# A four-layer graph network on one core: attention of twelve node tiles from a slot array, one one-hot of four on ScalarE, weights' sums by fours of node tiles

## The chip, the cores and the metric

One core of a Trainium2 chip runs the whole program as one launch. The metric is the device time of one execution in microseconds. Five engines work side by side: PE (matmuls; its weight loads are listed as PEld), DVE (VectorE), ACT (ScalarE), POOL (GpSimd) and SP (SyncE, which here only issues DMAs). Indirect gathers and stores (one row per partition, the row numbers taken from a column in SBUF) are issued from POOL, plain DMAs from SP and some from ACT.

## The reference

12,500 nodes with 96 features, 200,000 edges sorted by destination, 96 edge attributes. Four layers, each with a residual and a layer norm. Layers 0, 1 (two steps inside) and 3 sum rows of the source nodes over the edges of each destination; layer 2 is attention over edges with 8 heads of 12:

```python
x = _layernorm(x + _L0_gnn_ref(x, src, dst, ...))        # x@W_self + mean of x[src] @ W_neigh
x = _layernorm(x + _L1_gnn_ref(x, ..., src, dst))        # twice: sums of (x@W0)[src], then x / std
# _L2_gnn_ref:
Q_h, K_h, V_h = ((x @ Wq + bq), (x @ Wk + bk), (x @ Wv + bv))   # as (N, 8, 12)
E = (edge_attr @ We + be).reshape(-1, H, D)
score = K_h[src] * Q_h[dst] / sqrt(D) * E
score = exp(clip(score.sum(-1, keepdims=True), -5.0, 5.0))
wV = segment_sum(V_h[src] * score, dst);  Z = segment_sum(score, dst)
h_out = wV / (Z + 1e-06)
x = _layernorm(x + h_out)
x = _layernorm(x + _L3_gnn_ref(x, src, dst, ...))        # softmax-weighted sums of relu(x[src])
```

## The kernel before

**Tiles.** There are 98 node tiles of 128 nodes (`NB`) and 1563 edge tiles of 128 edges in the order of their destinations (`NT`). The edges of node tile d lie in the edge tiles `reach(d)`, 16d-6 to 16d+21.

**Two ways to sum over edges.** *By slots*: for the first 76 node tiles (`NS`) the first stage sorts each node tile's edges into 25 slot tiles of 128 places (`SQ`, 3200 places, `SD`), so that a group of 32 places holds edges whose sources all lie in one node tile. Source rows then come from a table in SBUF by matmuls with a one-hot `ohT` (four matmuls of 32 columns per slot tile, called granules), and a second one-hot `ohd` sums them into the node tile. 64 edges per node tile that do not fit are gathered as spare rows. Both one-hots are stored in DRAM (`ohT_d`, `ohd_d`) and loaded again by later passes. *By edges*: for the other node tiles POOL gathers source rows with an indirect DMA for each edge tile (`by_edges`, L1389), and one-hots made on DVE sum them.

**Stages.** (1) `passes`, first part: `edge_block` and `edge_steps` order the edges in 20 steps of 64 edge tiles, mostly on DVE; `first_sums` follows them, one node tile a turn (it makes and stores the one-hots, L1206 to L1225, gathers that tile's spare row on POOL, L1245, runs the granules on PE, L1302, and the sums, L1316); `by_edges` is advanced beside it. The framework's scheduler orders the instructions of this stage on each engine. (2), (3) Two `whole_pass` runs for the two steps of layer 1; the second also stores keys and values as f32 rows (`kv_d`) and queries as two f16 halves (`q_d`). (4) `attention`, wholly by edges. (5) `whole_pass` for layer 3, by slots for 68 node tiles, with its table of four f16 parts held in SBUF, where attention's `stage` writes it.

**Attention.** 391 units of four edge tiles. The order of work on PE, DVE, ACT and POOL is written out by hand (`manual_schedule`): round u asks for the key and value rows of unit u+8 (`ask`, L1631: four indirect gathers on POOL into one of 12 buffers `kv`), fetches the edge attributes and query rows of unit u+4 (SP), and does `score(u)`, `weigh(u-1)`, `terms(u-2)` with `one_hots_of(u-2)`, `queries(u+3)`, one step of the node stage, and `scatter(u-3)`. `score` has eight matmuls for the edge terms (f32, two passes, `ep`, L1669), eight for the queries (`qp`, L1673), two multiplications on DVE (`s`, L1677 and L1678) and the sum over each head (`sc`, L1680). `weigh` takes the exponential on ACT (L1689) and multiplies the values on DVE (`m`, L1692); with that a `kv` buffer comes free. `terms` splits the result into two f16 halves (`mh`, L1701, L1702); `one_hots_of` makes four one-hots of 256 columns on DVE (`ohe`, L1709); `scatter` sums into the node tiles (`acc`, L1725, seven matmuls a unit). `done` closes each node tile on DVE: the two halves' sum, the weights' sum, its reciprocal, a product (L1738 to L1743).

Of the kernel before, what the change touches and what calls it, by code (L numbers as in the profile page):

```python
# [11 lines left out]
F32 = mybir.dt.float32  # L12
# [11 lines left out]
P = 128  # L24
# [506 lines left out]
NS3 = 68  # L531
TS = 16 * NS + 8
# [10 lines left out]
def gnn_fast(  # L543
# [67 lines left out]
    kv_d = dram.tile([NB * P, 2 * D], F32, name="kv_d")  # L611
    q_d = dram.tile([(NB + 1) * P, 2 * D], F16, name="q_d")
# [192 lines left out]
    def l0_nodes(work, psum, pieces):  # L805
# [3 lines left out]
        for g, n in node_batches():  # L809
            xg = work.tile([P, GB, D], F32, name="x0", bufs=2)  # L810
# [11 lines left out]
            own = work.tile([P, GB, D], F32, name="own0", bufs=2)  # L822
# [32 lines left out]
    def edge_constants(big):  # L855
# [7 lines left out]
        c.first = big.tile([P, NT], BF16, name="first")  # L863
        c.cont = big.tile([P, NT], BF16, name="cont")
        c.same = big.tile([P, NT], BF16, name="same")
# [16 lines left out]
        with tc.tile_pool(name="s_ord", bufs=1) as ordp, tc.tile_pool(name="s_ordp", bufs=2, space=PSUM) as psum:  # L882
# [24 lines left out]
            last = ordp.tile([P, NT], F32, name="last")  # L907
            for j0 in range(0, NT, 512):
                n = min(512, NT - j0)
                for k, to in enumerate((c.first, last)):  # L910
                    p = psum.tile([P, 512], F32, name="p")
                    nc.tensor.matmul(p[:, :n], ones_f[0:1, :], ends[:, k, j0 : j0 + n], start=True, stop=True)
                    nc.vector.tensor_copy(to[:, j0 : j0 + n], p[:, :n])
            nc.vector.memset(c.cont[:, 0:1], 0.0)
            nc.vector.tensor_tensor(c.cont[:, 1:], c.first[:, 1:], last[:, : NT - 1], op=ALU.is_equal)
# [30 lines left out]
    def edge_block(c, blk, psum, b0):  # L946
# [27 lines left out]
        if slots:  # L974
# [4 lines left out]
            t.rearrange("t (f i) -> t f i", i=4), rowf[:, 1].rearrange("t i f -> t f i"),  # L979
# [65 lines left out]
        b.j = blk.tile([P, BL], F32, name="j")  # L1045
# [7 lines left out]
    def edge_steps(c, work, psum, t0):  # L1053
# [80 lines left out]
        pg_all = pb.rearrange("p k (g i) -> p k g i", i=UE)  # L1134

# [41 lines left out]

    def expand(work, psum, placed, d):
# [3 lines left out]
        p = psum.tile([SQ, P], F32, name="tp")  # L1182
        nc.tensor.transpose(p, lo[:, :SQ], ident)
        r = work.tile([SQ, P], BF16, name="lorow", bufs=2)
        nc.scalar.copy(r, p)
        nc.scalar.dma_start(rowd[d], r)
# [363 lines left out]
    def l1_stage(i):  # L1550
        def stage(work, psum, g, n, sums):
# [32 lines left out]
            nc.sync.dma_start(rows(kv_d, g, n), kv[:, :n, :])  # L1584
            nc.sync.dma_start(
# [6 lines left out]
    def attention():  # L1592
# [4 lines left out]
        CQ = 16  # L1597
        with ExitStack() as c2:
            cols, within = by_columns(c2.enter_context(tc.tile_pool(name="e_cols", bufs=1)), 0, NT, F32)
# [4 lines left out]
            accp = c2.enter_context(tc.tile_pool(name="e_acc", bufs=3, space=PSUM))  # L1604
            five = one.tile([P, per, HEADS], F32, name="five")
            nc.vector.memset(five, 5.0)
            wide = one.tile([P, 2 * P], BF16, name="wide")
            nc.gpsimd.iota(wide, pattern=[[1, 2 * P]], base=1, channel_multiplier=0, allow_small_or_imprecise_dtypes=True)
            attr = []
            for i in range(6):  # L1610
                t = one.tile([D + 1, per * P], F32, name=f"attr{i}")
                nc.vector.memset(t[D : D + 1], 1.0)
                attr.append(t)
            units = [(t0, min(per, NT - t0)) for t0 in range(0, NT, per)]
            blocks, got, asked, early, acc, held = {}, {}, {}, {}, {}, {}

            def ask_block(b):
                if b * CQ < NT:
                    n = min(CQ, NT - b * CQ)
                    qb = work.tile([P, CQ * P], BF16, name="qb")  # L1620
# [3 lines left out]
            def ask(u):  # L1624

                if u >= len(units):
                    return
                t0, n = units[u]
                kv = uw.tile([P, per, 2 * D], F32, name="kv", bufs=EARLY + 4)
                for i in range(n):  # L1630
                    nc.gpsimd.indirect_dma_start(  # L1631
                        out=kv[:, i, :], out_offset=None, in_=kv_d,
                        in_offset=bass.IndirectOffsetOnAxis(ap=cols[:, t0 + i : t0 + i + 1], axis=0),
# [3 lines left out]
            def fetch(u):  # L1637
# [4 lines left out]
                if t0 % CQ == 0:  # L1642
# [7 lines left out]
            def queries(u):  # L1650
# [4 lines left out]
                b = blocks[t0 // CQ][:, t0 % CQ * P : (t0 % CQ + n) * P]  # L1655
# [5 lines left out]

            def score(u):
                t0, n = units[u]
                a, qs = got.pop(u)
                ohq = asked.pop(u)
                kv = early.pop(u)
                ep = psum.tile([P, per, D], F32, name="ep")
                for i in range(n):
                    nc.tensor.matmul(ep[:, i, :], a[:, i * P : (i + 1) * P], w_e, start=True, stop=True)  # L1669
                qp = psum.tile([P, per, D], F32, name="qp")  # L1670
                for i in range(n):
# [4 lines left out]
                s = uw.tile([P, per, D], F32, name="s")  # L1676
                nc.vector.tensor_mul(s[:, :n, :], ep[:, :n, :], kv[:, :n, :D])  # L1677
                nc.vector.tensor_mul(s[:, :n, :], s[:, :n, :], qp[:, :n, :])  # L1678
                sc = uw.tile([P, per, HEADS], F32, name="sc", bufs=3)
                nc.vector.tensor_reduce(sc[:, :n, :], s[:, :n, :].rearrange("p e (h d) -> p e h d", d=HD), AX.X, ALU.add)  # L1680
                nc.vector.scalar_tensor_tensor(  # L1681
                    sc[:, :n, :], sc[:, :n, :], -5.0, five[:, :n, :], op0=ALU.max, op1=ALU.min
                )
                return n, kv, sc

            def weigh(n, kv, sc):
# [3 lines left out]
                m = uw.tile([P, per, HEADS, H1], F32, name="m")  # L1690
                nc.scalar.mul(m[:, :n, :, HD], ex[:, :n, :], 2.0**8)
                nc.vector.tensor_mul(  # L1692
                    m[:, :n, :, :HD], kv[:, :n, D:].rearrange("p e (h d) -> p e h d", d=HD),
                    ex[:, :n, :, None].to_broadcast([P, n, HEADS, HD]),
                )
                return n, m.rearrange("p e h d -> p e (h d)")

            def terms(n, m):
# [4 lines left out]
                return mh  # L1703

            def one_hots_of(u):
                t0, n = units[u]
                o = uw.tile([P, per, 2 * P], BF16, name="ohe")
# [284 lines left out]
```

## Time and profile before

| | us |
|---|---|
| median of 3 runs | 7493.61 (7463.65 to 7509.52) |
| profiled execution | 7481.49, its span 7479.0 |
| stage 1, with its start | 0 to 1541 |
| pass one, pass two | 1541 to 2550, 2550 to 3512 |
| attention | 3512 to 6098 |
| last pass | 6098 to 7479 |

The stage bounds are where the first and last instructions of each stage's lines start in the trace. Busy time of an engine counts when an instruction of it runs; matmuls overlap and their ends are modelled, so PE's busy time is not a measure of how full it is. A line of waits says which instruction waited, whose end released it, and then the total, the number and the longest of these waits. "issue" means that the profile shows nothing that was waited for, "remote" that the release can't be put down to an instruction.

### The profile page before, as it was taken

The numbers are of one execution on the slowest core, as the hardware profiler recorded it, in microseconds if no ns is written. First come the engines' busy times: TensorE is split into PE (matmuls) and PEld (weight loads), VectorE is DVE, ScalarE is ACT, GpSimd is POOL, SyncE is SP. The second block draws the span as 40 slices with busy tenths as digits, with TensorE's granted clock in tenths as the row PEclk, the third lists the DMA queues.
The fourth block names the chain that finished last, engine by engine and source line by source line (L and its number), as shares of the span: only waits on it lengthen the run. The fifth ranks groups of instructions, "written<-read, shape, count | busy, mean of one in ns | idle before, by whom it ended". The sixth has DMA issues, their size and how long they took to land.

```text
span 7479.0 us, 155826 instructions
## 1 busy us (share of the span) xinstructions
PE 4678.3 (63%) x63527; PEld 3383.4 (45%) x63527; DVE 4144.3 (55%) x9827; ACT 2805.1 (38%) x5549; POOL 3381.0 (45%) x3338
## 2 busy tenths in 40 slices
PE   5666666746667566676445555555555547777777
PEld 3455545534445444445344444444444434444344
DVE  7577777723334344445466666666666654454445
ACT  2455455522323223334234443334433433333334
POOL 0443454334343344332666656666665643334331
PEclk8677778767777777777565656655656558787788
DMA  4545455543333333344344444444444432233222
GB/s 106 155 162 167 147 173 166 169 107 101 105 101 110 102 109 113 108 119 140 111 124 131 126 125 130 127 127 128 127 129 126 127 91 87 88 91 87 87 88 66
DMA packets 656950, 894.03 MB, mean 120 GB/s; under 512 B 394162, under 2 KB 458885, under 8 KB 651357
## 3 DMA queue, kind: packets, MB, share of 16 engines
q1 hardware_dynamic: 498742, 615.02, 26.4%
q0 software_dynamic: 138784, 262.63, 13.2%
q8 instruction: 500, 8.19, 0.4%
q10 hardware_dynamic: 18695, 6.32, 0.4%
q14 instruction: 229, 1.88, 0.1%
HBM read 747.72 MB, written 135.87 MB: 118 GB/s over the span
## 4 chain that ended last, share of the span: by engine, by line
PE 31%; DVE 22%; another core or an unknown queue 17%; issue 16%; POOL 5%; ACT 4%; DMA 2%; DVEq 0%; ACTq 0%; SPq 0%; POOLq 0%
PE rows L1444 9%; PE acc L1455 8%; POOL kv L1631 5%; PE acc L1373 3%; DVE ohe L1709 3%; DVE msg L1447 2%; PE acc L1316 2%; DVE s L1678 2%; PE rows L1302 2%; DVE sc L1680 2%; DVE mh L1702 2%; DVE s L1677 2%; ACT msg L1306 1%; PE place L1166 1%
## 5 line engine op out<-in xcount | busy, mean ns | idle before, releaser
L1631 POOL DMA_INDIRECT kv<-kv_d,cols x1563 | 1543.3, 987 | 987.8 <-DVE m L1692 521.9
L1447 ACT CAST msg<-rows 128x384 f16<-128x384 f32 (+1 forms) x1440 | 876.7, 641 | 1810.6 <-remote 1110.7
L1444 PE MATMUL rows<-tab,ohT 128*32 128x192 f16 (+1 forms) x21560 | 1122.9, 294 | 677.6 <-issue 588.4
L1447 DVE CAST msg<-rows 128x768 f16<-128x768 f32 x720 | 687.3, 955 | 1486.7 <-remote 1027.4
L1389 POOL DMA_INDIRECT rows_e<-tab_d,cols x1065 | 1128.3, 1059 | 628.3 <-PE acc L1373 323.1
L1444 PEld LDWEIGHTS <-ohT 128*32 128x32 fp8e4 x21560 | 598.1, 101 | 1106.8 <-issue 1027.9
L1455 PE MATMUL acc<-msg,ohd 128*32 128x384 f16 (+1 forms) x10600 | 928.2, 323 | 260.1 <-issue 254.9
L1725 PE MATMUL acc<-mh,ohe 128*128 128x208 f16 x2727 | 516.1, 352 | 845.6 <-DVE ohe L1709 592.2
L1455 PEld LDWEIGHTS <-ohd 128*32 128x32 fp8e4 (+1 forms) x10600 | 558.8, 103 | 534.7 <-issue 441.3
L1725 PEld LDWEIGHTS <-ohe 128*128 128x128 bf16 x2727 | 294.3, 125 | 1008.3 <-DVE ohe L1709 648.0
L1669 PE MATMUL ep<-w_e,attr 97*128 97x96 f32 x3126 | 653.3, 378 | 22.9 <-issue 17.6
L1689 ACT ACTIVATE ex<-sc 128x32 f32<-128x32 f32 x391 | 89.6, 229 | 1477.9 <-DVE sc L1681 1255.6
L1389 POOL DMA_INDIRECT rows_e<-ex_d,cols x483 | 465.1, 963 | 384.8 <-PE acc L1373 246.2
L1669 PEld LDWEIGHTS ep<-w_e,attr 97*128 97x128 f32 x3126 | 621.6, 293 | 26.2 <-issue 13.3
L1673 PE MATMUL qp<-qs,ohq 128*128 128x96 f16 x3126 | 357.5, 258 | 345.1 <-issue 325.5
L1677 DVE TENSOR_TENSOR s<-ep,kv 128x384 f32<-128x384 f32 x391 | 216.1, 553 | 638.7 <-remote 446.6
L1306 ACT CAST msg<-rows 128x768 f16<-128x768 f32 x633 | 386.0, 644 | 428.8 <-PE rows L1302 186.3
L1316 PE MATMUL acc<-msg,ohd 128*32 128x194 f16 x7600 | 381.6, 291 | 242.3 <-ACT msg L1306 156.4
L1673 PEld LDWEIGHTS <-ohq 128*128 128x128 fp8e4 x3126 | 293.7, 134 | 396.6 <-issue 393.2
L1302 PE MATMUL rows<-tab,ohT 128*32 128x192 f16 x7448 | 395.2, 287 | 76.7 <-issue 74.9
L1245 POOL DMA_INDIRECT spare<-tab_d,spare_i x76 | 130.8, 1721 | 653.5 <-PE rows L1302 365.1
L1254 POOL DMA_INDIRECT spare<-tab_d,spare x76 | 72.4, 953 | 731.1 <-PE rows L1444 613.2
(695 smaller groups left out, 7566.9 us busy)
## 6 DMA issues: line engine op xcount, KB each, us to landing
ohT<-ohT_d SPq DMA_DIRECT2D x220, 400.0 KB
ohd<-ohd_d SPq DMA_DIRECT2D x220, 400.0 KB
attr<-cols_edge_attr_dram SPq DMA_DIRECT2D x390, 192.0 KB
bc<-rowd SPq DMA_DIRECT2D x76, 800.0 KB
qb<-qrow SPq DMA_DIRECT2D x97, 512.0 KB
sb<-srow SPq DMA_DIRECT2D x38, 1024.0 KB
ohd_d<-ohd SPq DMA_DIRECT2D x76, 400.0 KB
ohT_d<-ohT SPq DMA_DIRECT2D x76, 400.0 KB
```

Source lines behind the costliest of these rows:

```text
L1302: nc.tensor.matmul(ps[j * GR : (j + 1) * GR, i // R, i % R * W : (i % R + 1) * W], a, b, start=True, stop=True)
L1306: nc.scalar.copy(m[:, : n * R].rearrange("p (b r) t w -> p b (r t) w", r=R)[:, :, :, :D], ps[:, :n, : R * W].rearrange("p b (t w) -> p b t ...
L1316: nc.tensor.matmul(acc[d][j : j + GR, : W + 2], got[d][1][:, q, j : j + GR], m, start=(q == 0), stop=(q == SQ - 1))
L1389: nc.gpsimd.indirect_dma_start(out=m[:, i, :W], out_offset=None, in_=table, in_offset=bass.IndirectOffsetOnAxis(ap=rest_src[:, t : t + 1], ...
L1444: nc.tensor.matmul(ps[j * GR : (j + 1) * GR, i // R, i % R * W : (i % R + 1) * W], a, b, start=True, stop=True)
L1447: (nc.scalar.copy if engine else nc.vector.tensor_copy)(m, ps[:, :, : R * W])
L1455: nc.tensor.matmul(acc[d][j : j + wide, :W], got[d][1][:, q, j : j + wide], m, start=(q == 0), stop=(q == SQ - 1))
L1631: nc.gpsimd.indirect_dma_start(out=kv[:, i, :], out_offset=None, in_=kv_d, in_offset=bass.IndirectOffsetOnAxis(ap=cols[:, t0 + i : t0 + i ...
L1669: nc.tensor.matmul(ep[:, i, :], a[:, i * P : (i + 1) * P], w_e, start=True, stop=True)
L1673: nc.tensor.matmul(qp[:, i, :], ohq[:, i * P : (i + 1) * P], qs[:, t * D : (t + 1) * D], start=(t == 0), stop=(t == 1))
L1677: nc.vector.tensor_mul(s[:, :n, :], ep[:, :n, :], kv[:, :n, :D])
L1725: nc.tensor.matmul(acc[d].rearrange("p t w -> p (t w)"), ohe[:, i, k * P : (k + 1) * P], m[:, i].rearrange("p t w -> p (t w)"), start=(t = ...
```

## The change

- **Twelve node tiles by slots (`MS = 12`).** Attention's unit list becomes 345 edge units from edge tile 184 on, and 75 slot units of four slot tiles, spread evenly over them from the 16th edge unit to 24 before the end. A slot unit takes key and value rows (f16 halves) by granules from a table in SBUF, query rows by a one-hot made from a row of places' destinations, and edge terms from a slot array `es_d`.
- **The slot array.** The first stage fills `es_d` with zeros (three DMAs), works out each edge's place (`slot_i`), and after step 3 puts in, turn by turn, the edge terms of four of the first 198 edge tiles (`edge_terms`), with one indirect store per edge tile from POOL.
- **The table.** Pass two also stores keys and values as f16 halves (`kvh_d`); attention loads them into SBUF in its second round. That room was the last pass's table; so `stage` now stores the last pass's rows in DRAM alone while the slots last, and they are read back at the end (`bring`).
- **One-hots.** The first of each unit's four is made on ACT, as a square and a ramp; the other three stay on DVE.
- **Weights' sums.** Scaling, reciprocal and product move from `done` (once a node tile) into `stage` (once for four).
- **Buffers.** `kv` 12 to 11, `attr` 6 to 5, `qb` 3 to 2, edge accumulators 3 to 2, gather ring of the first stage 11 to 10; `ep` and `qp` share a tile. The columns of the last pass are loaded after attention. Edges stand in another order within a tile (by their number modulo four).

```diff
+    def edge_terms(c, work, psum):
+        last = reach(MS - 1)[1]
+        a = c.attr
+        nc.scalar.dma_start(a[:D, : UE * P], cols_attr[:, : UE * P])
+        for t0 in range(0, last + 1, UE):
+            yield
+            n = min(UE, last + 1 - t0)
+            p = psum.tile([P, UE, D], F32, name="tp")
+            for i in range(n):
+                nc.tensor.matmul(p[:, i, :], a[:, i * P : (i + 1) * P], w_e, start=True, stop=True)
+            e = work.tile([P, GB, D], F32, name="own0", bufs=4)
+            nc.scalar.copy(e[:, :n], p[:, :n])
...
+            for i in range(n):
+                st = nc.gpsimd.indirect_dma_start(
+                    out=es_d, out_offset=bass.IndirectOffsetOnAxis(ap=c.slot_i[:, t0 + i : t0 + i + 1], axis=0),
+                    in_=e[:, i, :], in_offset=None,
+                )
...
+            kvh = work.tile([P, GB, 2, 2 * D], F16, name="kvh")
+            halves_of(kv[:, :n, :], kvh[:, :n])
+            nc.sync.dma_start(rows(kvh_d, g, n), kvh[:, :n].rearrange("p g t w -> p g (t w)"))
...
-            units = [(t0, min(per, NT - t0)) for t0 in range(0, NT, per)]
+            edges = [(t0, min(per, NT - t0)) for t0 in range(first_t, NT, per)]
+            units, made, many = [], 0, MS * SQ // UE
+            for i, e in enumerate(edges):
+                units.append(e)
+                while made < many and (made + 1) * (len(edges) - HEAD - TAIL) <= (i + 1 - HEAD) * many:
+                    units.append((made * UE, None))
+                    made += 1
...
+            def ask_spare(d):
+                if d < MS:
+                    t = su.tile([P, 4 * D], F16, name="spare")
+                    nc.gpsimd.indirect_dma_start(out=t, out_offset=None, in_=kvh_d, ...)
+                    sp[d] = sp[d + 1] = t
...
-                kv = uw.tile([P, per, 2 * D], F32, name="kv", bufs=EARLY + 4)
+                kv = uw.tile([P, per, 2 * D], F32, name="kv", bufs=EARLY + 3)
...
+            def score_slots(u):
...
+                        for t in range(2):
+                            for j, (x, y) in enumerate(pairs):
+                                nc.tensor.matmul(
+                                    kvp[j * GR : (j + 1) * GR, i // 2, i % 2 * 2 * D : (i % 2 + 1) * 2 * D], x,
+                                    y[:, t * 2 * D : (t + 1) * 2 * D], start=(t == 0), stop=(t == 1),
+                                )
+                        for t in range(2):
+                            nc.tensor.matmul(
+                                qp[:, i, :], ohq[:, i * P : (i + 1) * P], ql[d][:, t * D : (t + 1) * D],
+                                start=(t == 0), stop=(t == 1),
+                            )
...
                 for i in range(n):
-                    nc.vector.tensor_scalar(o[:, i], wide, within[:, t0 + i : t0 + i + 1], None, op0=ALU.is_equal)
+                    at = less_within[:, t0 + i - first_t : t0 + i - first_t + 1]
+                    if i == 0:
+                        nc.scalar.activation(o[:, i], wide, AF.Square, bias=at)
+                        nc.scalar.activation(o[:, i], o[:, i], AF.Relu, bias=1.0, scale=-1.0)
+                    else:
+                        nc.vector.tensor_scalar(o[:, i], less_wide, at, None, op0=ALU.is_equal)
...
+                for i, (d, q, oh) in enumerate(places or ()):
+                    if q == 0:
+                        acc[d] = slotp.tile([P, 2, W], F32, name="acc")
+                    nc.tensor.matmul(acc[d]..., oh, m[:, i]..., start=(q == 0), stop=(q == SQ - 1))
+                    if q == SQ - 1:
+                        done(d, acc.pop(d), "slots")
...
-                nc.vector.tensor_scalar(z, sh[:, :, HD:], 2.0**-8, 1e-6, op0=ALU.mult, op1=ALU.add)
-                nc.vector.reciprocal(z, z)
...
+            def stage(g, n, both):
+                x2 = load_rows(one, x_d[1], g, n, "x_in")
+                sh = both[:, :n, :].rearrange("p g (h d) -> p g h d", d=H1)
+                z = one.tile([P, GB, HEADS, 1], F32, name="z")
+                nc.vector.tensor_scalar(z[:, :n], sh[:, :, :, HD:], 2.0**-8, 1e-6, op0=ALU.mult, op1=ALU.add)
+                nc.vector.reciprocal(z[:, :n], z[:, :n])
...
+                    if u == 1:
+                        kept["kv"] = load_table(tabp, kvh_d)
+                    if u == final:
+                        kept[2] = new_table(tabp, 4 * D, F16)
+                    if u > final + 2 and stored:
+                        bring()
...
+                    if k < MS // 4:
+                        to = es_d[4 * k * SD : 4 * (k + 1) * SD].rearrange("(p r c) w -> p r (c w)", p=P, c=2)
+                        nc.sync.dma_start(to, none[:, None, :].to_broadcast([P, 2 * SQ, 2 * D]))
+                    if k == MS // 4:
+                        next(terms_of)
                     while turn <= min(4 * k, NS - 2):
                         next(sums)
                         turn += 1
+                        if k > MS // 4:
+                            next(terms_of, None)
```

## The prediction

> **What bounds the kernel now.** I read the page first, then a table of the five stages, then the waits of the attention stage, and then short windows that set PE against POOL. The profiled execution spans 7479.0 us (7481.5 with what lies around it); the median of the three runs shown is 7493.6, 0.16% above it. The sum below is made against 7481.5. About 1% is what a measurement of this kernel can tell from no change.
>
> Stages, in order: the first sums with the edge ordering, pass one, pass two, attention, the last pass.
>
> ```profile
> PE 4678.3 (63%) x63527; PEld 3383.4 (45%) x63527; DVE 4144.3 (55%) x9827; ACT 2805.1 (38%) x5549; POOL 3381.0 (45%) x3338
> 230.00:1541.00 1311.00, 888.42 (x18326) 663.89 (x18325) 918.70 (x1989) 678.62 (x1083) 577.05 (x430) 0.76 0.50 162
> 1541.00:2550.00 1009.00, 646.49 (x10566) 463.54 (x10555) 380.16 (x781) 287.52 (x569) 402.05 (x422) 0.75 0.38 105
> 2550.00:3512.00 962.00, 648.32 (x10311) 443.97 (x10310) 426.94 (x880) 311.37 (x697) 353.09 (x367) 0.76 0.39 113
> 3512.00:6098.00 2586.00, 1366.71 (x8987) 1149.60 (x8991) 1615.13 (x4576) 1005.68 (x2128) 1543.81 (x1564) 0.59 0.43 125
> 6098.00:7479.00 1381.00, 1004.02 (x14726) 570.00 (x14715) 633.99 (x1165) 456.47 (x787) 497.33 (x517) 0.80 0.29 86
> ```
>
> Columns: window, length, then busy time and count of PE, PEld, DVE, ACT, POOL, then granted clock, DMA share, GB/s. No engine is full anywhere. In attention (2586 us, 391 units of four edge tiles, 6.6 us each) DVE is busy 62% and POOL 60%. So the waits decide:
>
> ```profile
> L1631 POOL DMA_INDIRECT kv<-kv_d,cols x1480 | 1461.6, 988 | 945.0 <-DVE m L1692 512.2 <-issue 413.5 <-DVE sc L1681 7.9
> ...
> POOL kv L1631 <- DVE m L1692: 512.2, 117, 10.9
> POOL kv L1631 <- issue: 413.5, 1335, 1.1
> DVE s L1677 <- remote: 424.8, 62, 17.1
> ```
>
> In the 2400 us from 3600 on, POOL's gathers and their issue gaps take 1461.6 + 413.5 = 1875 us, 1.267 us for each of 1480; the rest is 117 waits for a free kv buffer (4.38 us each, one every 3.17 units). POOL's queue thus accounts for attention. Why is the buffer late? Two stretches, one in pass one, one in attention, each beginning with a run of gathers on POOL:
>
> ```profile
> 1812.40:1817.00 4.60, 4.18 (x67) 3.58 (x65) 3.06 (x8) 0.26 (x1) 3.69 (x4) 1.00 0.57 183
> 1817.00:1833.60 16.60, 5.04 (x29) 2.18 (x26) 1.81 (x5) 1.28 (x2) 12.63 (x14) 0.64 0.20 51
> 1836.00:1845.00 9.00, 8.13 (x136) 5.79 (x136) 7.13 (x16) 4.86 (x10) 0.00 (x0) 0.66 0.38 114
> ...
> 4707.20:4717.30 10.10, 9.30 (x62) 8.50 (x63) 8.73 (x26) 6.22 (x13) 7.91 (x8) 0.56 0.52 150
> 4717.30:4722.50 5.20, 0.90 (x11) 0.45 (x9) 0.56 (x1) 0.00 (x0) 3.96 (x5) 0.72 0.42 116
> ```
>
> While POOL issues gathers back to back, PE gets some 65 matmuls further and then crawls: 29 in 16.6 us, against 136 in 9.0 us with POOL quiet. It recovers about 2 us after the last gather. So the engines take turns: POOL bursts (12 gathers, 15 us), PE crawls, DVE has no scores, no kv buffer comes free, POOL stops, PE runs, DVE frees a buffer. A gather costs the kernel wherever PE has work, and the first stage shows the price. A turn is one node tile there (from its spare-row matmul to the next one's); four turns in a row:
>
> ```profile
> 718.00:730.60 12.60, 9.39 (x275) 7.97 (x271) 12.60 (x20) 7.72 (x11) 4.07 (x1) 0.82 0.94 311
> 730.60:741.50 10.90, 7.71 (x215) 6.77 (x211) 10.32 (x32) 7.66 (x10) 2.35 (x1) 0.69 0.71 244
> 741.50:761.50 20.00, 16.51 (x307) 13.31 (x301) 17.23 (x41) 11.01 (x17) 4.82 (x4) 0.91 0.30 109
> 761.50:788.30 26.80, 12.74 (x210) 8.42 (x213) 11.60 (x33) 8.37 (x16) 15.18 (x14) 0.68 0.26 73
> ```
>
> Turns with one gather last 11 to 13 us, with 14 they last 26.8. Over all turns after 300 us, counted from the trace's list: 31 with up to two gathers (mean 1.0) last 12.7 us, 17 with three to six (4.8) last 16.2, eleven with twelve or more (13.2) last 26.3. That is 0.91 us per gather over the first step and 1.12 over all.
>
> **The change, part by part.** *Removed in attention.* The unit list begins at edge tile 184, so 1563 gathers become 1379, and six gathers of spare rows are added: 178 fewer. 178 x 1.267 = -226 us of POOL's queue. With them go 46 units and their 46 / 3.17 x 4.38 = 64 us of waits.
>
> *Added in attention: 75 slot units*, one after about every fourth edge unit. Each takes no kv gather, but on PE has 32 matmuls for key and value rows, 8 for queries and 4 for the sums: 44, against 23 in an edge unit (8 ep, 8 qp, 7 acc). The waits come once per 3.17 x 23 = 73 matmuls. After: (345 x 23 + 75 x 44) / 73 = 154 waits; before: 391 x 23 / 73 = 123. So +31 x 4.38 = +136 us (this holds the -64). Low end: slot units run while POOL is busy and add no wait, +136 becomes -64. High end: each is one more DVE iteration of 4.1 us (that is what one lasts in a burst), 75 x 4.1 = 308, so -64 + 308 = +244; at the whole 6.6 us of a unit, +431. I take +136, since matmuls in a burst are what the windows show to be rationed.
>
> *A wait that it adds.* The spare rows for node tiles d+2, d+3 are gathered into one of two buffers, on POOL, at fetch time, four units ahead. The buffer is freed by PE's last granule of tile d-1, which for d = 2, 6, 10 lies in the very unit fetched for. Behind this gather stand all further kv gathers, and DVE waits for those. POOL may lose its lead of up to nine units five times; meanwhile PE runs uncrawled, and afterwards a long burst follows. Bounds 0 and 5 x 22 us (POOL's turn of five units at 4.4 us); I take +40. The slots' one accumulator makes PE wait for DVE's reduction at the nine tile ends that fall inside a unit, 0 to 9 x 4.1 us: +10. At the start, a 9.6 MB table comes in (12,544 packets of 768 B at 36 ns over 16 engines, 28 us) under POOL's first burst, which shrinks from 56 gathers (93 us until PE gets going) to some 44: -15 to +30, taken as 0. Attention: -226 + 136 + 40 + 10 = -40.
>
> *Moved or shortened on DVE.* One of four one-hots goes to ACT: 345 x 0.300 = 104 us off DVE; on ACT two instructions of 256 columns, some 0.46 us each (between 229 ns at 32 columns and 717 at 512, rows L1689 and L1658), 315 us more, 3.5 us of each 6.6 us unit. The sums by fours save 98 x (0.205 + 0.203 + 0.258) us less about 24, 41 us. Both cost and bring nothing: DVE is idle 0.38 of the stage, waiting for crawling PE. If that cover were gone, DVE's 4.1 us iteration would be the pace and they would bring 145 us, until ACT's 3.5 us is next.
>
> *Added in the first stage.* The edge terms of 198 tiles: 50 units with an attr load and four tiles of f32 matmuls each, one ACT copy (0.5 us), and 198 indirect stores on POOL into the slot array. In POOL's order they stand in fours among the row gathers and spare gathers, so what queues behind them is the next spare row, which PE's last granule of a node tile needs. No indirect store is in the trace; the nearest row is the gather on the same queue. At 0.91 to 1.12 us: 180 to 222, and since the fours lie in turns that have 5.6 gathers on average already, I take 1.0: +198. Low end: lone bursts of four in the two passes cost PE 2.4 us, 0.6 each, 119; high end 1.3 each, as in bursts of 24, 257. The 396 f32 matmuls (pitch 0.11 us at full clock, 0.21 at half) exceed what the gathers' own matmuls hold in that price by 12 to 51: +20.
>
> The Trainium skill (SBUF — State Buffer, "Who interferes with whom") says that DMA never contends with a compute engine and that PE and ACT never wait on anyone. The windows above speak against it for POOL's gathers; by that rule the 198 would fall away and the sum would be 7482. The same skill (DMA: Bandwidth & Descriptors, "Specifications") says that transfers under 512 B are read-modify-write, and the stores have rows of 384 B; no row here shows such a scatter, and even at double the 22 ns of a 384 B packet 25,344 rows would take 70 us of 16 engines that are half idle, so the sum stays.
>
> *Elsewhere.* Three zero fills of 4.9 MB at the start (19,200 packets x 39 ns / 16 = 47 us of DMA beside DVE work): 0 to 47, +10. Half-precision keys and values in pass two: 25 x about 1 us on ACT and DVE, both under half busy: 0 to 25, +5. Columns of the last pass now load after attention: its first gathers come some us later, +5. The table of the last pass is reloaded in 23 pieces during the 24 tail units: 0.
>
> **Sum:** 7481.5 + 198 + 20 - 40 + 20 = 7679.5.
>
> **Rivals.** *Short bursts are nearly free, so the change is faster.* Slot units break POOL's bursts and scatters come in fours; if the crawl needs a long burst, the waits do not rise (-290 in attention) and the scatters cost 119: 7481.5 - 290 + 119 + 20 + 20 = 7350. For it: single gathers in the passes cost PE 0.3 us. Against: fours cost 2.4. It decides once a slot unit costs under 0.75 us and a scatter 0.6: then it is over 1% faster. *It evens out:* attention falls by 290, the first stage keeps its price: 7481.5 - 290 + 218 + 20 = 7430, within 1%. *A slot unit is one more full DVE iteration:* 7481.5 - 226 + 244 + 50 + 218 + 20 = 7788. For it: DVE sets the pace between crawls (4.1 us an iteration). Against: a slot unit has no one-hots, about 3 us.
>
> **How the numbers follow.** Forecast 0.50, its own range 7560 to 7780. Short bursts free 0.18 (7350). Even 0.14 (7430). Full iteration 0.18 (7788 and above). The time is the forecast's, 7680. The range runs from 7410, past the even case, to 7860; about 0.16 lies below and a little above. Faster 0.18, same 0.14, slower 0.68.
>
> **What would show it.** First stage 218 to 240 us longer, POOL with 198 more DMA instructions there, turns of 15 to 17 us where they carry four more; attention within 100 us of 2586 with some 150 waits of POOL for DVE's m, DVE's busy share lower. It is wrong if the stores leave the turns at 12 to 13 us, or if POOL's waits in attention fall in number.

## The result, and the profile after

The changed kernel takes 7694.49 us (median of four runs, 7682.82 to 7717.56) against 7484.75: ratio 1.0283, 95% interval 1.0241 to 1.0324. It is slower, where 7680 was predicted (+198 on the profiled run; its span grew by 210.7, from 7479.0 to 7689.7). Each experiment was run in a set together with the kernel before, and in four sets that kernel took 7485, 7486, 7488 and 7404 us ("crawling" below), in two it took 5323 and 5335 ("free"), so every number is compared within its set or between the sets of 7485 to 7488.

The page's line and the stages after, in the columns of the table of stages before:

```profile
PE 4901.6 (64%) x66165; PEld 3446.4 (45%) x66165; DVE 4116.1 (54%) x9318; ACT 3117.1 (41%) x6459; POOL 3423.1 (45%) x3358
0.00:345.00 345.00, 156.15 (x928) 119.36 (x928) 258.40 (x584) 67.29 (x292) 6.65 (x38) 0.71 0.51 148
345.00:1840.00 1495.00, 975.47 (x18483) 720.80 (x18481) 849.76 (x1905) 699.61 (x1131) 797.07 (x629) 0.73 0.47 150
1840.00:2840.00 1000.00, 641.44 (x10504) 460.82 (x10505) 372.88 (x758) 285.77 (x566) 399.48 (x419) 0.74 0.38 105
2840.00:3806.00 966.00, 648.52 (x10305) 445.53 (x10305) 441.17 (x899) 327.82 (x714) 354.75 (x368) 0.76 0.42 121
3806.00:6311.00 2505.00, 1482.83 (x11221) 1123.34 (x11219) 1556.42 (x4000) 1279.52 (x2968) 1367.20 (x1387) 0.62 0.48 136
6311.00:7689.70 1378.70, 997.17 (x14727) 576.52 (x14727) 637.43 (x1174) 457.13 (x789) 497.96 (x517) 0.80 0.30 86
```

Cut by the first and last instructions of PE's granules and POOL's gathers, the 210.7 us lie here:

| us | before | after | change | predicted |
|---|---|---|---|---|
| start, to the first granule | 228 | 345 | +117 | +10 (fills) |
| turns of the first stage | 1313 | 1486 | +173 | +218 |
| passes one and two, with the gap ahead | 1941 | 1953 | +12 | +5 |
| attention, up to the last pass | 2616 | 2528 | -88 | -40 |
| last pass | 1382 | 1378 | -4 | +5 |

Attention by POOL's groups and waits (busy time, mean; then idle time and what ended it; below, total, number and longest of each wait), first before, over the whole stage, then after:

```profile
L1631 POOL DMA_INDIRECT kv<-kv_d,cols x1563 | 1543.3, 987 | 987.8 <-DVE m L1692 521.9 <-issue 437.6 <-DMA cols<-cols_src_dram 8.7
...
POOL kv L1631 <- DVE m L1692: 521.9, 119, 10.9
POOL kv L1631 <- issue: 437.6, 1414, 1.1
```

```profile
L1736 POOL DMA_INDIRECT kv<-kv_d,cols x1379 | 1358.5, 985 | 1030.8 <-DVE m L1847 632.1 <-issue 364.9 <-DVE s L1834 6.7
...
POOL kv L1736 <- DVE m L1847: 632.1, 149, 10.3
POOL kv L1736 <- issue: 364.9, 1184, 1.5
POOL spare L1694 <- PE qp L1800: 42.4, 4, 21.5
```

Gathers and their gaps fell from 1543.3 + 437.6 = 1980.9 us to 1358.5 + 364.9 = 1723.4, the waits for DVE's m rose from 521.9 us (119) to 632.1 (149), and the new gather of spare rows waited 42.4 us.

Four turns in a row of the first stage; they carry, by the trace's list, 13, 9, 3 and 18 indirect DMAs, of which 0, 4, 2 and 10 are stores:

```profile
900.80:924.60 23.80, 15.91 (x259) 11.66 (x248) 13.90 (x47) 12.85 (x17) 13.04 (x13) 0.73 0.50 145
924.60:941.30 16.70, 11.97 (x227) 8.73 (x230) 9.73 (x26) 6.25 (x16) 12.00 (x10) 0.81 0.48 142
941.30:957.80 16.50, 14.59 (x338) 11.46 (x329) 15.09 (x40) 11.73 (x22) 2.76 (x3) 0.96 0.78 239
957.80:988.30 30.50, 20.00 (x255) 14.01 (x247) 13.45 (x25) 9.11 (x14) 21.82 (x19) 0.64 0.46 146
```

A store lengthens a turn as a gather does: by the same list, turns with up to two gathers and no store last 11.2 us (19 of them, 0.9 gathers on average), those with up to two gathers and at least one store 15.4 (14 of them, 1.0 gathers and 3.9 stores on average; single ones from 8.4 to 23.7).

### The profile page after: what moved, and what is told of

Same layout as the page of the kernel before. It is cut to its first block, busy times and chain, and to the rows that moved or that the text cites. A ratio compares the mean times of both kernels' runs of the same rounds, so it can differ in the third digit from the quotient of the medians.

```text
span 7689.7 us, 161813 instructions
## 1 busy us (share of the span) xinstructions
PE 4901.6 (64%) x66165; PEld 3446.4 (45%) x66165; DVE 4116.1 (54%) x9318; ACT 3117.1 (41%) x6459; POOL 3423.1 (45%) x3358
## 4 chain that ended last, share of the span: by engine, by line
PE 36%; issue 19%; DVE 17%; another core or an unknown queue 13%; POOL 6%; ACT 5%; DMA 3%; SPq 0%; ACTq 0%; DVEq 0%; POOLq 0%
PE rows L1490 9%; PE acc L1501 7%; POOL kv L1736 6%; PE acc L1419 4%; PE acc L1362 2%; PE rows L1348 2%; DVE msg L1493 2%; PE acc L1901 2%; PE eq L1827 2%; DVE mh L1859 1%; DVE sc L1811 1%; ACT msg L1352 1%; PE tp L1573 1%; DVE s L1835 1%
## 5 line engine op out<-in xcount | busy, mean ns | idle before, releaser
L1736 POOL DMA_INDIRECT kv<-kv_d,cols x1379 | 1358.5, 985 | 1030.8 <-DVE m L1847 632.1
L1435 POOL DMA_INDIRECT rows_e<-tab_d,cols x1065 | 1091.5, 1025 | 565.8 <-issue 271.4
L1901 PE MATMUL acc<-mh,ohe 128*128 128x208 f16 x2397 | 462.3, 343 | 375.5 <-DVE mh L1859 153.5
L1827 PE MATMUL eq<-w_e,attr 97*128 97x96 f32 x2758 | 577.3, 372 | 160.3 <-issue 140.3
L1827 PEld LDWEIGHTS eq<-w_e,attr 97*128 97x128 f32 x2758 | 535.5, 284 | 210.9 <-issue 176.3
L1362 PEld LDWEIGHTS <-ohd 128*32 128x32 fp8e4 x7600 | 221.4, 110 | 345.1 <-issue 330.4
L1834 DVE TENSOR_TENSOR s<-eq,kv 128x384 f32<-128x384 f32 x345 | 190.7, 553 | 345.3 <-remote 208.1
L1419 PE MATMUL acc<-rows_e,ones_e 128*128 128x192 f16 (+2 forms) x2644 | 351.3, 286 | 33.5 <-issue 20.5
```

The source lines that it names most:

```text
L1362: nc.tensor.matmul(acc[d][j : j + GR, : W + 2], got[d][1][:, q, j : j + GR], m, start=(q == 0), stop=(q == SQ - 1))
L1419: nc.tensor.matmul(acc[:, : W + count], ones[:, :, i], rows_of[u][:, t % UE + i, : W + count], start=(t + i == first), stop=(t + i == last),)
L1435: nc.gpsimd.indirect_dma_start(out=m[:, i, :W], out_offset=None, in_=table, in_offset=bass.IndirectOffsetOnAxis(ap=rest_src[:, t : t + 1], ...
L1736: nc.gpsimd.indirect_dma_start(out=kv[:, i, :], out_offset=None, in_=kv_d, in_offset=bass.IndirectOffsetOnAxis(ap=cols[:, t0 + i - first_t ...
L1901: nc.tensor.matmul(acc[d].rearrange("p t w -> p (t w)"), ohe[:, i, k * P : (k + 1) * P], m[:, i].rearrange("p t w -> p (t w)"), start=(t = ...
```

## The experiments

The theory: PE is starved while POOL issues indirect DMAs, so each store costs about 1 us, each slot unit brings waits by its matmuls, and DVE's and ACT's share does not matter. ("PE crawls" is short for the stretches of the prediction in which PE gets few matmuls beside POOL's gathers; a "four" is the four stores of one unit of edge terms.) The rivals are stated with each run. The late first granule, 117 us, was not in the prediction; two causes were set against each other.

**1. Unchanged kernels, and what the crawl is.**

> The kernel before, unchanged, for its trace. In the last four runs it took 5323 us on another chip than the one of the first profile (7485): there the two passes took 1109 us instead of 1927, and POOL's 149 waits for DVE's m in attention were gone. If this run is on such a chip: PE does not crawl beside POOL's gathers, attention is POOL's queue alone, 1563 x 1.30 us = 2035 us from first to last gather, the passes 1110, the last pass 850, the turns of the first stage about 1050. If it is on a chip as the first: the stages of the first profile again (1313, 1914, 2522, 1382) within 2%. If the difference lies in the chip's state and not in PE's feeding, all stages would differ by one factor.

> The changed kernel, unchanged. Where PE does not crawl: attention 1563 - 1379 = 184 gathers x 1.30 = 239 us shorter, the start 117 longer, the turns some 95 longer for the stores: within 30 us of before, 5310 to 5350. Where it crawls: 7690 against 7485 as before.

Both fell in a crawling set. Before: span 7478.9, turns 1308, passes 1915, kv gathers 2525 from first to last. After: 7702.76, ratio 1.0292 (1.0275 to 1.0309). So the profiles repeat within a few us, and "before" has no trace in a free set. The changed code does: here are 24 us with POOL issuing gathers throughout. The first three lines are of the repeated changed kernel (crawling set): the middle of a burst in pass one, then the first 24 us of pass two, then the last 16 of these. The next are of own_rings, whose code is the same from pass one on (free set): the same two stretches of pass two, then attention:

```profile
1942.00:1966.00 24.00, 5.27 (x29) 1.66 (x28) 2.47 (x4) 0.00 (x0) 18.01 (x20) 0.54 0.31 65
...
2808.50:2832.50 24.00, 8.29 (x94) 4.46 (x94) 0.96 (x1) 1.76 (x3) 18.21 (x20) 0.50 0.54 135
2816.50:2832.50 16.00, 5.34 (x30) 1.98 (x29) 0.04 (x1) 0.48 (x1) 12.04 (x14) 0.50 0.31 73
```

```profile
2021.00:2045.00 24.00, 21.03 (x531) 16.96 (x531) 10.47 (x13) 12.66 (x22) 18.03 (x20) 0.91 0.91 258
2029.00:2045.00 16.00, 13.82 (x371) 11.06 (x359) 7.59 (x10) 8.61 (x16) 12.04 (x14) 1.00 0.85 256
...
2610.00:4409.00 1799.00, 1290.84 (x11180) 1027.71 (x11181) 1534.37 (x3951) 1264.84 (x2939) 1377.27 (x1384) 0.69 0.67 187
```

At the start of pass two POOL issues 20 gathers in both (18.2 and 18.0 us busy), and PE gets 94 matmuls in one and 531 in the other; in the last 16 us 30 and 371. In the free set both passes last 1108 us instead of 1930, and attention (last line) is POOL's queue alone: 1379 gathers in 1799 us, 1.30 each, with 10 us of waits for m:

```profile
L1736 POOL DMA_INDIRECT kv<-kv_d,cols x1379 | 1371.9, 995 | 425.5 <-issue 326.3 <-DMA kv<-kv_d,cols 16.8 <-DVE sc L1812 12.5
```

This is the sharpest support for the prediction's reading: where PE does not crawl, the waits that it counted are gone. It does not show why PE crawls; the last section says what is known of that.

**2. The late start: shared ring or zero fills?** `own_rings`:

```diff
-            xg = work.tile([P, GB, D], F32, name="own0", bufs=4)
+            xg = work.tile([P, GB, D], F32, name="x0", bufs=2)
-            own = work.tile([P, GB, D], F32, name="own0", bufs=4)
+            own = work.tile([P, GB, D], F32, name="own0", bufs=2)
-            e = work.tile([P, GB, D], F32, name="own0", bufs=4)
+            e = work.tile([P, GB, D], F32, name=("own0", "x0")[t0 // UE % 2], bufs=2)
```

> The first stage's node rows and their products get rings of two buffers each again (edge terms alternate between the two); all else as in the changed kernel. In the changed kernel the first granule starts at 345 us, before at 228 us: 117 us that the prediction did not have. Theory A, the shared ring of four buffers is the cause (each load of node rows waits until an older product has been stored): the first granule comes back to 230 to 250 us, and the time falls by 80 to 117 us, to 7580 to 7615. Theory B, the three zero fills of 4.9 MB are the cause (they stand on SP's queue ahead of the first loads and fill the DMA engines): the first granule stays after 320 us, the time within 25 us of 7694. A middle case: the delay goes, but the turns, which were short after the late start (11.2 us with one gather against 12.7 before) grow back, and less than half of the 117 us is won.

`rings_late` adds to it:

```diff
-                    if k < MS // 4:
-                        to = es_d[4 * k * SD : 4 * (k + 1) * SD]...
+                    if 3 <= k < 6:
+                        to = es_d[4 * (k - 3) * SD : 4 * (k - 2) * SD]...
-                    if k == MS // 4:
+                    if k == 6:
...
-                        if k > MS // 4:
+                        if k > 6:
```

> As own_rings, and the three zero fills are issued three steps later (with the fourth to sixth step of the ordering instead of the first to third), the edge terms after them. Theory A: within 20 us of own_rings, since the ring alone was the cause. Theory B: the first granule falls to 230 to 250 us only here, and the time is 80 to 117 us below own_rings.

Both fell in the free set of 5323. own_rings: 5288.58, ratio 0.9939 (0.9922 to 0.9955); rings_late: 5275.83, 0.9905 (0.9887 to 0.9923). The first granule comes at 238 and 261 us; with the shared ring, in the same set, at 344 (kernel half below). So the ring is the cause, and the fills are not: issued later, they left the first granule no earlier, and the whole became 13 us shorter. But the turns grew back, from 1139 us (half) to 1196: the middle case. The same in a crawling set, `rings_noact` (own rings, and in attention `if i == 0` for ACT's one-hot never taken, all four on DVE):

> Own rings for node rows and products in the first stage, and all four one-hots of an edge unit on DVE again (345 x 0.288 = 99 us back on DVE, 345 x 0.924 = 319 us off ACT); read apart by stage. Where PE crawls: the first granule comes at 240 instead of 346 us, and the turns stay at 1483 (7590) or grow back by some 60 us as they did without the crawl, since DVE's ordering has less of a lead (7650); attention stays at 2432 within 15 us, since DVE waits for PE there: the prediction's nothing. The rival: DVE's iteration sets the pace between crawls, and attention grows by 40 to 100 us. Where PE does not crawl attention is POOL's queue, 1800 us, and 5288 stands within 15 us.

7668.24, ratio 1.0246 (1.0224 to 1.0268). Turns and attention in the repeated changed kernel, then in rings_noact:

```profile
346.00:1829.00 1483.00, 961.90 (x18433) 714.46 (x18432) 843.35 (x1882) 699.13 (x1128) 795.03 (x629) 0.75 0.48 150
3827.00:6259.00 2432.00, 1435.27 (x10997) 1089.53 (x10997) 1501.21 (x3861) 1244.23 (x2880) 1362.64 (x1384) 0.63 0.50 137
```

```profile
240.00:1798.00 1558.00, 1005.73 (x18884) 744.11 (x18888) 957.46 (x2092) 703.01 (x1142) 819.45 (x627) 0.72 0.49 154
3797.00:6232.00 2435.00, 1465.17 (x10992) 1106.74 (x10993) 1565.90 (x4200) 984.57 (x2213) 1367.15 (x1384) 0.61 0.50 137
```

The start is 106 us earlier and the turns 75 us longer, since 114 us more of DVE work and some 450 more matmuls lie in them: during a late start the ordering of the edges runs ahead. That shows in the DMA issues of the start, `sb` being the rows that an ordering block loads; the repeated changed kernel up to its first granule, then rings_noact:

```profile
sb<-srow SPq DMA_DIRECT2D x12, 1024.0 KB
```

```profile
sb<-srow SPq DMA_DIRECT2D x4, 1024.0 KB
```

So the shared ring costs 31 us net, not 117 (in the free set 49: 344 to 238, less 1139 to 1196). And in attention 65 us of DVE's busy time and 260 of ACT's change hands for 3 us: in a crawling set the one-hot on ACT is worth nothing, as predicted.

**3. The stores.** In `no_store`, `range(n)` around the store becomes `range(0)`.

> The 198 indirect stores of the first stage are left out, so the slot array holds zeros and the attention of twelve node tiles is computed from them; the edge terms' loads, f32 matmuls and copies stay. The prediction's step (a store costs 1.0 us in a turn, bounds 0.6 and 1.3): 198 us less, 7496, between 7437 and 7575. A fit over the changed kernel's turns gives 1.23 us for each store and 9.1 us for an empty turn: by it 244 us less, 7450. Rival, the turns are longer for the f32 matmuls and the delay of the start, and the stores are hidden: less than 60 us, above 7634.

> The kernel of no_store once more, for a chip on which PE crawls beside POOL's indirect DMAs (the changed kernel 7695 there). The prediction: 198 stores at 1.0 us, 198 us less, 7497, and between 7440 (1.3 each) and 7575 (0.6 each). The fit over the changed kernel's turns on that chip, 1.25 us a store and 9.2 us for an empty turn: 248 us less, 7447. Rival, from pass1, where the turns without any store lasted 1343 us against 1483 with them: 140 us less, 7555. On a chip without the crawl 5231 again.

Both fell in free sets: 5230.9 and 5233.25, ratios 0.9829 (0.9813 to 0.9846) and 0.9809 (0.9793 to 0.9825). The turns last 1044 us against half's 1139: 95 us, 0.48 us a store, below the prediction's bounds (0.6 to 1.3) and above the rival's 60 us in all. The turns of half, then of no_store, each with POOL's waits for PE's granules there:

```profile
344.00:1483.00 1139.00, 818.97 (x18426) 655.87 (x18428) 841.11 (x1882) 691.68 (x1128) 859.84 (x629) 0.82 0.61 195
...
POOL spare L1291 <- PE rows L1348: 33.9, 19, 12.5
```

```profile
345.00:1389.00 1044.00, 811.09 (x18429) 653.03 (x18424) 836.50 (x1881) 691.37 (x1128) 624.74 (x431) 0.85 0.64 203
...
POOL spare L1291 <- PE rows L1348: 147.6, 28, 15.4
```

PE's matmuls and busy time are nearly the same in both, and with the stores POOL's spare gathers wait 114 us less for PE. This reads as POOL's own queue setting more of the pace in the free set, so that a store costs something there without PE's crawl. For a crawling set the edit went into `no_store_half`, together with the edit of 4:

> Both edits at once, read apart by stage: the 198 stores are left out of the first stage, and slot units take the first f16 half of keys and values alone (1200 matmuls fewer). On the chip on which PE crawls (7695): the turns of the first stage, 1483 us, become 1285 by the prediction's 1.0 us a store (1230 by the fit's 1.25, 1343 by pass1's turns); attention's gathers, 2432 us from first to last, become 2362 with some 133 waits of POOL for DVE's m if a slot unit is charged by its matmuls, and stay with 149 if it is charged as a unit. Sum of the two steps: 7695 - 198 - 70 = 7427; of the rivals: 7555. On a chip without the crawl: turns 1044, attention 1800, 5230.

```profile
345.00:1677.00 1332.00, 919.20 (x18434) 695.28 (x18432) 841.01 (x1881) 695.38 (x1128) 540.94 (x431) 0.77 0.51 159
3674.00:6088.00 2414.00, 1338.05 (x9798) 1059.94 (x9799) 1501.33 (x3861) 1240.44 (x2880) 1363.96 (x1384) 0.62 0.50 138
```

7514.95, 1.0036 (1.0019 to 1.0053). Turns 1331 (from first to last granule) against 1483 at the same start and with the same DVE work: 152 us, 0.77 us a store. The fit over turns (1.25) put too much on the stores, probably because it hands them what the fours share with their matmuls and loads. A store costs about a quarter less than the prediction's 1.0, within its bounds; how much of the 0.77 is PE's crawl and how much POOL's queue, as in the free set, is not separated.

**4. Is a slot unit charged by its matmuls?** `half`:

```diff
-                        for t in range(2):
+                        for t in range(1):
                             for j, (x, y) in enumerate(pairs):
...
-                                    y[:, t * 2 * D : (t + 1) * 2 * D], start=(t == 0), stop=(t == 1),
+                                    y[:, t * 2 * D : (t + 1) * 2 * D], start=True, stop=True,
```

> Slot units take the first f16 half of keys and values alone: 16 of their 44 matmuls are left out, 1200 in all (values lose their low half). The prediction charges a slot unit by its matmuls, one wait of POOL (4.2 us) for 73 matmuls: 16 waits fewer, 149 to about 133, and 70 us less, 7625. Rival, a slot unit is an iteration of DVE and costs the same with half of its matmuls: 149 waits stay, 7680 to 7710.

> The kernel of half once more (1200 of the slot units' 3300 matmuls left out), for a chip on which PE crawls. The prediction's charge of one wait of 4.2 us for 73 matmuls: 149 waits of POOL become about 133, 70 us less, 7625. Rival, a slot unit costs as a unit: 7680 to 7710. On a chip without the crawl attention is POOL's queue and 5335 stands again.

In the free sets it shows nothing, since attention is POOL's queue: 5335.32 (1.0025, 1.0016 to 1.0035) and 5338.73 (1.0009, 0.9998 to 1.0021), kv gathers 1800 us from first to last as in own_rings. These two are also the nearest thing to the changed kernel in a free set, which was not run there itself: by them the change is worth about nothing there. In the crawling set the second line of no_store_half's table answers: 2414 us against 2432, and in its waits

```profile
POOL kv L1736 <- DVE m L1847: 620.3, 143, 10.3
```

against 151 (637.3 us) in the repeated changed kernel. Eight waits fewer, not sixteen, and 18 us, not 70. Neither theory holds whole, and eight is not far above the spread of kernels with all of these matmuls (148 to 153 waits in four profiles). At before's rate (119 waits for 391 units) 345 edge units would bring 105, so some 46 of the 151 fall to the slot units; leaving out 36% of their matmuls takes 8 of these 46 away. The rest goes with the unit, or with its other matmuls, or with the ring of 11 `kv` buffers instead of 12, which may have changed the edge units' rate and was not tried alone.

**5. The stores elsewhere.** `pass1` has own rings and moves `edge_terms` into the first whole pass, with an attr buffer and a ring of two for its products there:

```diff
+            terms_of = edge_terms(c, work, psum) if c else iter(())
+            next(terms_of, None)
             for i in range(0, len(items), 5 * R):
+                if i // (5 * R) % 3 == 1:
+                    next(terms_of, None)
```

> Own rings for node rows and products again, and the edge terms (50 attr loads, 396 f32 matmuls, 198 stores in fours) move out of the first stage into the first whole pass, one four after every third group of ten slot tiles. Where PE does not crawl: the first stage loses 0.48 us a store, 95 us (that is what leaving the stores out brought, 95 of the turns' 1139); in the pass POOL is busy for two thirds and PE for nine tenths, so theory A, PE's 396 f32 matmuls and what stands behind them cost 50 to 90 us and nothing is won (5250 to 5290); theory B, they are hidden, 5190 to 5220. Where PE crawls: a lone burst of four costs 2.4 us in the pass, 50 of them 119 us, against 173 us more in the turns of the first stage, and the start is 117 us shorter: 7694 - 117 - 173 + 119 = 7523, or 7580 if the turns grow back as the start comes earlier.

Crawling set: 7754.71, 1.0358 (1.0341 to 1.0375), slower than the changed kernel. Both passes in the repeated changed kernel, then here, and POOL's group of the stores here:

```profile
1855.00:3785.00 1930.00, 1282.84 (x20719) 896.02 (x20722) 796.53 (x1608) 603.21 (x1244) 754.24 (x787) 0.75 0.42 112
```

```profile
1622.00:3839.00 2217.00, 1437.31 (x21121) 1005.91 (x21117) 799.11 (x1604) 629.03 (x1295) 946.62 (x982) 0.73 0.39 107
...
L1214 POOL DMA_INDIRECT es_d<-terms,slot_i x198 | 195.2, 986 | 370.3 <-ACT terms L1209 321.4 <-issue 48.6 <-DMA es_d<-terms,slot_i 0.3
```

287 us more for 50 fours, 5.7 us each where the expectation had 2.4. One reason is in the line: POOL holds the stores back for ACT's copy (321 us of waits, with the gathers queued behind it); how the rest divides between longer bursts and the terms' matmuls, loads and the edit's own buffers is not shown. The run gives something else: its first stage, with an equal start (243 us against 240), lasts 1343 us in turns without edge terms,

```profile
243.00:1586.00 1343.00, 903.98 (x18482) 672.28 (x18485) 951.39 (x2093) 684.70 (x1092) 596.07 (x429) 0.76 0.51 162
```

and rings_noact's 1558 with them. All of the edge terms cost 215 us there.

**6. The spare gather's wait.** `rings_late_spare3` is rings_late with `bufs=3` for attention's `spare` rows.

> Three of the changed kernel's side costs taken away at once, read apart by stage: own rings for node rows and products, the zero fills three steps later, and a third buffer for attention's spare rows, so that their gather on POOL need not wait for PE. Where PE crawls (changed kernel 7695, with own rings 7668): start 240 to 265 and turns 1558 or, if the zero fills beside the first loads cost something, up to 30 us fewer over both; POOL's four waits of 42 us in all for the spare buffer vanish. The prediction's step takes them as a loss of 40 us: attention's gathers 2432 become 2392. Rival: while POOL waits there PE runs uncrawled and POOL would have waited for DVE's m instead, so attention stays at 2432 within 10 us and the waits for m grow. Sum 7600 to 7630, or 7640 to 7670. Where PE does not crawl: 5276 within 10 us, attention 1805 unchanged; below the kernel before (5323 to 5335) by 1%.

The set of 7404: 7579.84, ratio 1.0232 (1.0200 to 1.0263). Start and turns sum to 1769 us (rings_noact 1798, in a set 1.1% slower, so the late fills are worth some 10 to 20). kv gathers take 2389 us, and POOL's waits are

```profile
POOL kv L1736 <- DVE m L1847: 641.0, 153, 10.2
POOL kv L1736 <- issue: 362.4, 1186, 1.2
```

The four waits of 42 us are gone and those for m have hardly grown (637.3 us, 151, before the edit): 43 us fewer, 42 of them by POOL's account the waits. That speaks for the prediction's step against the rival, but does not settle it: the set is faster, by 1.1% in the kernel before and by 0.7% in the two passes (1917.5 us against 1930), which over 2432 us would be 16 to 27 us, and no kernel with two spare buffers was run in it. It is the lowest ratio of the changed kernel in a crawling set, and still 2.3% behind the kernel before; in a free set rings_late is 1% ahead of it. No version here was shown to beat the kernel before in both kinds of sets.

## Why the prediction was right, step by step

- **Bound and mechanism: right as far as the runs go.** In the crawling sets PE gets 94 matmuls beside 20 gathers, in the free ones 531 with the same code, and there the change costs about nothing. What links the gathers to PE is open, and the price of a store is not the crawl's alone: 0.48 us of it is there in the free set too.
- **Stores +198, matmuls +20:** right as a sum, 215 us by experiments 2 and 5 at equal start; its parts are off. The stores alone are 152 (0.77 each), which leaves some 63 for loads, f32 matmuls, copies and their waits, if the two differences, taken at different starts, may be combined. The prediction had 20 for the matmuls, by their pitch alone, and nothing for the copies.
- **Start, zero fills +10: the step that failed.** With own rings the first granule comes at 240 to 243 us (rings_noact, pass1) against 228, so at most some 15 us of the start are the fills'. What was missed is an edit that neither the list of buffer changes nor the sum names: the node rows' tile (`xg`), which had a ring of two of its own, joins the products' ring. That delays the first granule by 106 us and, as DVE's ordering then runs ahead, costs 31 net. Another 35 of the turns (1343 in pass1 against 1308 before), with no store or edge term in them, were not foreseen either; which of the slot numbers on DVE, the second row of `expand` and the gather ring of 10 they belong to, no run separates. Together, 215 + 35, less the 75 that the late start takes out of the turns, make the 175 by which the turns grew in the repeated pair (1308 to 1483).
- **Attention -40, measured -88.** Gathers -257, or -250 with the six gathers of spare rows, instead of -226: 184 fewer x 1.267 is 233, and each of the rest took 1.250. Waits +110 instead of +136: 149 of 154 foreseen, at 4.24 us instead of 4.38. Spare gather 42 of 40, with experiment 6 in its favour. The slots' accumulator was given 10; PE did wait for it (25.9 us in six waits), but in POOL's account it is not seen: there all other waits between the first and the last gather grew by 8 (19.6 to 27.5), and in the repeated pair by nothing. The number of waits came out by a rule, so many matmuls per wait, that experiment 4 bears out by half: eight waits went with the 16 matmuls where the rule has sixteen, and what the other waits hang on stays open. That 149 came so near 154 is partly luck.
- **One-hot on ACT, nothing:** right (3 us in a crawling set). The sums by fours were not tried alone.
- **The total is better than its steps.** First stage 290 instead of 228, attention 48 lower than forecast: +62 and -48 nearly cancel, so the 15 us between forecast and result owe much to luck.

Of the signs that the prediction named, the 150 waits are there, attention is within 100 us, and turns with stores last 15.4 us on average. The first stage became 290 us longer instead of 218 to 240: that sign failed, by the late start. DVE's busy share in attention, which was to be lower, hardly moved (1615 of 2586 us, now 1556 of 2505): its work and the stage shrank alike.

The Trainium skill (SBUF — State Buffer, "Who interferes with whom") says, in a rule on SBUF's ports, that DMA never contends with a compute engine and that PE never waits on anyone. The free sets agree with it (531 matmuls beside 20 gathers). In the crawling ones PE gets 94 at the same place; whether it is held up at SBUF, of which the page speaks, no run shows.

## What to carry to other kernels

Price an indirect DMA by what the engines beside it lose, read from stretches of the same trace with few and with many of them, and expect it to vary with where it stands: among the turns a store with its share of loads and matmuls cost 1.1 us (215 for 198), in a pass 1.45 (287), and in the free set the stores alone 0.48 where in the crawling one they cost 0.77. Go through a diff's buffer counts and names as through its instructions: two tiles that come to share a ring wait for each other. And when a stage starts late, look at what ran ahead in the meantime before the whole delay is called a loss.

## What the runs showed of the hardware

The same program runs 40% longer in some sets than in others (the kernel before 7486 against 5323), and the difference is not one factor: passes 1930 against 1108 us, the turns 1483 against 1139, the start 346 against 344. The granted clock (0.70 to 0.74 against 0.77 to 0.85) goes with it, but at the start of pass two it is 0.50 against 0.91 while PE's matmuls are 94 against 531. Attention's gathers take 0.985 and 0.995 us. What starves PE there is not shown by any record; the loads of instructions, the first suspect, arrive in both kinds of sets (520 packets of 16 KB, 1.07 and 1.05 us each), one of them in the middle of the crawl in pass one above (at 1955.6 us) without ending it. Two of the sets, one free and one crawling, bear the same chip number, so it may not be a property of the chip.
